# Cross-attention block: keys spread by two transfers, heads interleaved on even and odd partitions, three evictions on ScalarE, rows of the step in a new order

## The chip, the core and the metric

The kernel runs on one core of a Trainium2 chip. The metric is the device time of one execution in microseconds, and of several executions the median.

## The reference, cut to what matters

It is one transformer block with cross-attention, in float32. `x` (queries) and `ctx` (keys and values) have the shape 128 x 128 x 256: 128 batch rows, each with 128 tokens of width 256. There are 16 heads of width 16.

```python
q = (x @ Wq + bq).reshape(b, s, 16, 16).transpose(0, 2, 1, 3)
k = (ctx @ Wk + bk).reshape(b, s, 16, 16).transpose(0, 2, 1, 3)
v = (ctx @ Wv + bv).reshape(b, s, 16, 16).transpose(0, 2, 1, 3)
scores = einsum('bhqd,bhkd->bhqk', q, k) / sqrt(16)
scores = where(j < i, scores, -1e30)          # i query, j key
attn = softmax(scores, axis=-1)
attn[:, :, 0, :] = 0.0                        # query 0 has no keys
o = einsum('bhqk,bhkd->bhqd', attn, v).transpose(0, 2, 1, 3).reshape(b, s, 256)
x = layer_norm(x + o @ Wo + bo, ln1_g, ln1_b)
out = layer_norm(x + relu(x @ W1 + b1) @ W2 + b2, ln2_g, ln2_b)   # W1 256x1024
```

None of the biases and layernorm parameters is trivial.

## The kernel before

The 128 batch rows are taken two at a time: 64 pairs, each with 256 tokens. A pair passes through a pipeline some four steps long, so that one step works on the scores of pair p, on the context of pair p-2 or so, and on the feed-forward layers of pairs p-3 and p-4. Pairs 0 to 6 and the last are written out as special steps; all others run the same list, `ORDER`.

`ORDER` is a string of keys, written by hand. `step(p)` goes through it and calls, for each key, the piece of code behind it; `key-1` means that the piece is for pair p-1 of that count. Every engine executes its own instructions in exactly the written order and waits by semaphores for what it needs. So the list sets what stands ahead of what on each of TensorE (PE), VectorE (DVE), ScalarE (ACT), GpSimd (POOL) and on the DMA queue of SyncE (SP).

The dense products are made by a scheme with seven products of halves in place of eight (the class `Seven`). In the keys of the list a letter names the product and a digit which of its seven: `v` values, `o` attention output, `q` queries, `k` keys, `h` the first feed-forward layer, `w` the second. With a letter in place of the digit the key is an eviction of that product: `kk`/`kk2` keep a finished part (ACT), `ka`/`kb` add one bank to what was kept (DVE), `kr` is the rest, one 128x128 piece. `hk`/`hk2`/`hk5`, `ha`, `hb`, `hf` are the same for the first layer, and `re0` to `re3` and `ro0` to `ro3` its relu pieces. Each product has a fixed PSUM bank: first layer 0, 1, 2; keys 3; values 4; output 5; second layer 6; queries 7.

The attention of one step runs so:

- `scores` (L428): for all 16 heads of a pair, both batch rows, on TensorE in strips of 32 partitions. Only the blocks on and under the diagonal are made; the "high" halves (queries 64 to 127) go to banks 0 to 3, the "low" halves to banks 4 to 7.
- `mask...`, `max...`, `lowmax`, `eh...`, `el...`: mask, negated maxima (L1873, L1879), exponentials by head on ACT (L920), into `sm`.
- `turn0`, `turn1`, `turn2` (L521): the softmax weights are transposed in 32x32 blocks by DVE into the buffer `turned`, three instructions in a step. `turni` (L504) adds the inverse sums and `turnx` (L1935) blocks of x.
- `br0` to `br3`, `bring` (L540): sixteen DMAs of 128 KB on SP's queue move the blocks from `turned` to `brought`, each to the partitions where it belongs.
- `weigh` (L574, L584): the weights in `brought` by the values, on TensorE in banks 7 and 5; then `context` (L600) multiplies by the inverse sums, which also lie in `brought`, and ends the use of that buffer. The next pair's `bring` waits for it, and the next `turn` waits until `bring` has read `turned`.

The keys of a pair leave the product as `kr`, a tile with partition = feature (2 x 128 features), token along the free dimension. A strip of 32 partitions holds two heads, and the scores need each head by itself. So `spread` makes a tile `kT` in two halves: the even half with the odd heads set to zero, the odd half with the even heads set to zero. Both are made by multiplying `kr` with a column of zeros and ones, `half`: the even half by ACT (`ks`, L1267) and the odd half by POOL (`ks2`, L1272). The tile `kT` comes from a rotating pool.

Other lines that are named below: L1216 and L1221 `qa`, `qb` (queries, DVE), L1226 `qr`, L1243 the ACT evictions of keys, L1262 `kr`, L1256 and L1259 `ka` and `kb`, L1311 `vr` (last piece of the values), L1327 joins of a product with what was kept (`wr`, `wa` and others), L499 `recip`, L1908 `means`, L691 and L728 the normalizations on ACT and POOL (`norm1`, `norm2`), L753 `store` of the output, L92 and L99 the loads of tokens (`load`: four DMAs, `loadx`: one DMA of 512 KB every second step).

Of the kernel before, what the change touches and what calls it, by code (L numbers as in the profile page):

```python
# [19 lines left out]
def tile_cross_attention_block(  # L20
# [106 lines left out]
    wk = weight(Wk, "wk")  # L127
    wq = weight(Wq, "wq")
    c_first = loads.tile([P, 4, D], F32, tag="cb2", name="c_first", bufs=2)
    nc.scalar.dma_start(c_first[:, 0:2], c[0:2].rearrange("b p d -> p b d"))  # L130
    bk_c = column(bk, "bk_c")
    bq_c = column(bq, "bq_c")
# [50 lines left out]
    half4 = const.tile([P, 2, NS], F32, tag="half4", name="half4")  # L183
    half = const.tile([P, 2], F32, tag="half", name="half")
    nc.gpsimd.memset(half4, 1.0)
    for e in range(2):
        nc.gpsimd.affine_select(
            out=half4[:, e, :], in_=half4[:, e, :], compare_op=ALU.is_ge, fill=0.0,
            base=-DK * e, pattern=[[-32, NS]], channel_multiplier=1,
        )  # L190
        nc.gpsimd.affine_select(
            out=half4[:, e, :], in_=half4[:, e, :], compare_op=ALU.is_ge, fill=0.0,
            base=DK * e + DK - 1, pattern=[[32, NS]], channel_multiplier=-1,
        )
    nc.vector.tensor_reduce(half, half4, AX.X, ALU.add)
# [16 lines left out]
    WIDTH = (H + HH) * 32  # L212
    ROW = WIDTH + 2 * P
    turned_all = const.tile([P, NS * ROW + P], F32, tag="turned", name="turned")
# [108 lines left out]
    def project_keys(p, at=0):  # L323
        st = states[p]
        st["kT"] = proj.tile([P, KC, 2, TP], F32, tag="kT", name=f"kT_{p}")
        st["pk"] = project(wk, st["cT"], at_bank(at, f"pk_{p}") if p > 3 else bank(f"pk_{p}"), 6 if p < 2 else 0)
# [83 lines left out]
    def scores_both(p):  # L410
# [26 lines left out]
    def mask(p, hi, rs):  # L437
# [3 lines left out]
        if not hi and rs[0] == 0 and "both" in st:  # L441
            r = rs[0]
            at = (6, 4)[r // 2]
# [747 lines left out]
    class Queries(Seven):  # L1191
# [33 lines left out]
        def rest(self):  # L1225
            nc.vector.tensor_scalar(  # L1226
                self.q[:, 0, P:], self.a, QSCALE, bqs_c[:, 0:1], ALU.mult, ALU.add
            )

    class Keys(Seven):  # L1230

        def __init__(self, p, at):
            st = states[p]
            self.k = proj.tile([P, KC, TP], F32, tag="kr", name=f"kr_{p}", bufs=1)
            self.kT = st["kT"] = proj.tile([P, KC, 2, TP], F32, tag="kT", name=f"kT_{p}")
# [25 lines left out]
        def rest(self):  # L1261
            nc.vector.tensor_scalar(  # L1262
                self.k[:, 0, P:], self.a, bk_c[:, 0:1], None, ALU.add
            )

        def spread(self):
            nc.scalar.activation(  # L1267
# [1082 lines left out]
```

## Time and profile before

| | |
|---|---|
| median of 3 runs | 1527.7 us (1525.65 to 1528.93) |
| the profiled execution | 1528.17 us |
| its span | 1526.0 us, mean granted TensorE clock 0.993 |
| busy PE / weight loads | 1488.0 us (98% of the span) / 1415.2 us (93%) |
| busy DVE | 1410.1 us (92%) |
| busy ACT | 1299.1 us (85%) |
| busy POOL | 1320.8 us (87%) |
| DMA queue of SP | 61.7% of 16 engines' span, 199.58 MB |

The span is the time from the first to the last instruction that the profile has; the execution's own time holds 2.2 us more. The busy times of the engines overlap, and all are near the span: no engine is idle for long, so an average over the span does not tell which of them sets the pace. For that the prediction goes to one turn of the step and reads who waits for whom. In its rows a time in front is the start in us from the span's start, the number after it the busy time of the group, and `[0.18 <-DVE hT L1411]` says that the engine had waited 0.18 us, at the end of which that instruction released it. `<-` between tiles reads "made from".

### The profile page before, as it was taken

What the parts mean: (1) busy time and instruction counts of PE and PEld (TensorE: products, weight loads), DVE (VectorE), ACT (ScalarE), POOL (GpSimd) and SP (SyncE); (2) the same over time, 40 slices, a digit from 0 to 9 for tenths busy, and PEclk for the clock granted to TensorE, in tenths of its full rate; (3) what the DMA queues carried; (4) which work ended last, traced back from release to release, by engine and by line L of the source; (5) the groups of instructions that cost most, each with busy time, mean ns of one, the idle gap of its engine ahead of it and who ended that gap; (6) DMA issues with size and microseconds to landing.
All of it is one profiled execution on the core that took longest, in us unless ns stands there. A gap on an engine that the chain in (4) does not pass through costs nothing.

```text
span 1526.0 us, 56681 instructions
## 1 busy us (share of the span) xinstructions
PE 1488.0 (98%) x20711; PEld 1415.2 (93%) x20711; DVE 1410.1 (92%) x3397; ACT 1299.1 (85%) x5445; POOL 1320.8 (87%) x1877
## 2 busy tenths in 40 slices
PE   9999899999999999999999999999999999999898
PEld 7887799999999999999999999999999999999888
DVE  7987899999999999999999999999999999999577
ACT  6567798998998998998998998998998999999553
POOL 6876698998998998998998998998898898998767
PEclk9999899999999999999999999999999999999999
DMA  8366566766676766776766776666666666675251
GB/s 199 85 123 127 129 147 128 151 133 135 145 150 128 148 134 132 148 152 126 149 134 133 146 148 132 146 134 138 141 146 136 144 134 138 141 151 126 52 141 49
DMA packets 351298, 205.30 MB, mean 135 GB/s; under 512 B 277808, under 2 KB 319024, under 8 KB 351024
## 3 DMA queue, kind: packets, MB, share of 16 engines
q1 hardware_dynamic: 348736, 199.58, 61.7%
q8 instruction: 166, 2.72, 0.8%
q10 hardware_dynamic: 2288, 2.11, 0.6%
q14 instruction: 108, 0.88, 0.2%
HBM read 55.06 MB, written 18.09 MB: 48 GB/s over the span
## 4 chain that ended last, share of the span: by engine, by line
PE 79%; DVE 8%; POOL 4%; ACT 3%; SPq 2%; issue 2%; DMA 2%; DVEq 0%; POOLq 0%; ACTq 0%
PE banks L1175 40%; PE banks L1392 22%; PE banks L428 7%; PE banks L584 3%; DVE hT L1411 3%; PE banks L574 2%; SPq L540 2%; DVE turned L521 2%; ACT sm L920 1%; PE banks L858 1%; PE banks L960 1%; DMA brought<-turned 1%; PE banks L1072 1%; PE banks L288 1%; POOL sm L464 1%
## 5 line engine op out<-in xcount | busy, mean ns | idle before, releaser
L920 ACT ACTIVATE sm<-banks,nmx 128x128 f32<-128x128 f32 x944 | 355.2, 415 | 28.4 <-DVE nmx L1879 19.4
L920 ACT ACTIVATE sm<-sm,nmx 128x64 f32<-128x64 f32 x944 | 330.6, 425 | 0.0
L920 ACT ACTIVATION_READ_ACCUMULATOR sm<-sm,nmx 128x1 f32 x944 | 261.3, 277 | 0.0
L920 ACT ACTIVATION_READ_ACCUMULATOR sm<-banks,nmx 128x1 f32 x944 | 240.0, 254 | 0.0
L521 DVE STREAM_TRANSPOSE turned<-sm 128x1024 f32<-128x1024 f32 x186 | 226.1, 1219 | 7.8 <-DMA brought<-turned 5.7
L1868 POOL TENSOR_TENSOR hS<-hT 128x512 f32<-128x512 f32 x112 | 142.7, 1274 | 45.4 <-ACT hT L1433 26.6
L1175 PE MATMUL banks<-wt,hS 128*128 128x128 f32 x1344 | 177.7, 276 | 0.8 <-POOL hS L1868 0.8
L1392 PE MATMUL banks<-xS,w1t 128*128 128x128 f32 x1344 | 178.2, 276 | 0.0
L1175 PEld LDWEIGHTS banks<-wt,hS 128*128 128x128 f32 x1344 | 163.6, 192 | 1.0 <-POOL hS L1868 1.0
L1392 PEld LDWEIGHTS banks<-xS,w1t 128*128 128x128 f32 x1344 | 163.4, 192 | 0.0
L1879 DVE TENSOR_REDUCE nmx<-banks 128x4 f32<-128x512 f32 x224 | 146.1, 672 | 0.0
L1433 ACT ACTIVATE hT<-banks,b1e_c 128x256 f32<-128x256 f32 x168 | 72.4, 465 | 75.3 <-DVE hT L1431 54.5
L428 PE MATMUL banks<-kT,qT 32*64 32x128 f32 (+1 forms) x3840 | 118.8, 336 | 4.8 <-issue 2.3
L1392 PE MATMUL banks<-brought,w 128*128 128x128 f32 x896 | 118.4, 276 | 0.0
L428 PEld LDWEIGHTS banks<-kT,qT 32*64 32x64 f32 x3840 | 93.8, 132 | 20.7 <-issue 5.2
L1175 PE MATMUL banks<-w,hT 128*128 128x128 f32 x896 | 109.7, 276 | 2.2 <-DVE t L1327 1.9
L1272 POOL TENSOR_TENSOR kT<-kr,half 128x512 f32<-128x512 f32 x56 | 58.2, 1040 | 59.8 <-ACT hT L1433 41.3
L1392 PEld LDWEIGHTS banks<-brought,w 128*128 128x128 f32 x896 | 109.0, 192 | 0.0
L1175 PEld LDWEIGHTS banks<-w,hT 128*128 128x128 f32 x896 | 104.7, 192 | 2.7 <-DVE t L1327 2.1
L1421 ACT ACTIVATE hT<-hT,b1e_c 128x256 f32<-128x256 f32 x224 | 95.6, 497 | 1.4
L1873 DVE TENSOR_TENSOR banks<-banks,neg 128x256 f32<-128x256 f32 x224 | 89.9, 425 | 0.7 <-PE banks L428 0.4
L1900 DVE BATCH_NORM_STATS2 bsa<-t 128x6 f32<-128x256 f32 x224 | 83.2, 414 | 0.0
(330 smaller groups left out, 4936.9 us busy)
## 6 DMA issues: line engine op xcount, KB each, us to landing
brought<-turned SPq DMA_DIRECT2D x936, 128.0 KB, 2.4
out_dram<-t SPq DMA_DIRECT2D x63, 256.0 KB, 2.4
xb<-in_x_dram SPq DMA_DIRECT2D x124, 128.0 KB, 4.8
cb<-in_ctx_dram SPq DMA_DIRECT2D x124, 128.0 KB, 3.7
x<-in_x_dram SPq DMA_DIRECT2D x31, 512.0 KB, 4.2
brought<-turned SPq DMA_DIRECT2D x40, 96.0 KB, 2.2
w<-in_L_xattn_W_dram SPq DMA_DIRECT2D x2, 1024.0 KB, 8.1
brought<-turned ACTq DMA_DIRECT2D x8, 128.0 KB, 4.3
```

The costliest lines, as they stand in the source:

```text
L428: nc.tensor.matmul(st["sps", hi][r][s * HP : (s + 1) * HP, m * 2 * n : (m + 1) * 2 * n].rearrange("p (e j) -> p e j", e=2), st["qT"][strip ...
L521: nc.vector.transpose(turned[:, :, at : at + 256].rearrange("p j (n a) -> p n j a", a=32), states[p]["sm", hi].rearrange("p h j -> p (h j) ...
L920: nc.scalar.activation(sm[:, h, :], src, AF.Exp, bias=nmx[:, h : h + 1], scale=1.0, **({"accum_out": st["su"][:, at : at + 1]} if summed e ...
L1175: nc.tensor.matmul(out, left(k) if self.depth > 1 else left, right(k) if self.depth > 1 else right, start=(n == 1 and k == 0), stop=(k == ...
L1272: nc.gpsimd.tensor_tensor(self.kT[:, :, 1, :], self.k, half[:, 1:2, None].to_broadcast([P, KC, TP]), ALU.mult)
L1392: nc.tensor.matmul(ps[:, i * P : (i + 1) * P].rearrange("p (n a) -> p n a", a=32), left(i), right, start=(n in (1, 2, 5) and i == 0), stop ...
L1421: nc.scalar.activation(self.hT[:, f, at], self.hT[:, f, at] if src is None else src, AF.Relu, bias=b1e_c[:, f : f + 1], scale=1.0,)
L1433: nc.scalar.activation(out, src, AF.Relu, bias=bias, scale=1.0)
L1868: nc.gpsimd.tensor_tensor(c[:, n], left, right, how)
L1873: nc.vector.tensor_tensor(ps[:, :, HP:], ps[:, :, HP:], neg[:, 1, None, :].to_broadcast([P, 4, HP]), ALU.add)
L1879: nc.vector.tensor_reduce(states[p]["nmx", 1][:, 4 * b : 4 * b + 4], banks[:, b].rearrange("p (n j) -> p n j", j=P), AX.X, ALU.max, negate ...
L1900: nc.vector.bn_stats(states[p]["bs", p][:, at + s], states[q][t][:, s])
```

## The change

**Heads interleaved.** The weights Wk and Wq are loaded into a staging space (in `turned_all`, free at that time) and copied by ACT with their columns permuted, so that the two heads of a strip no longer stand on 16 partitions each but on the even and the odd partitions. The biases bk and bq are permuted by a small matmul with a permuted identity, `mixing`. `half` now is a column for the even and one for the odd partitions, made from the identity.

**Keys spread by two transfers.** `kT` is one of two fixed tiles, `kTs`, in turn. `ks` and `ks2` are no longer instructions of ACT and POOL; each is a DMA on SP's queue, which copies every second partition of `kr` to the same partitions of its half of `kT`. The partitions in between are not written.

**Three evictions to ScalarE.** `qr`, `kr` and `vr` go from DVE to ACT.

**Strips and masks.** The low halves of strip r go to bank 4 + r (before: 6, 7, 4, 5), and the eight groups of the scores are issued in another order of strips. The low halves of strips 0 and 1 are masked one by one (`maskA0`, `maskA1`) and those of 2 and 3 together (`maskB`), where it was the other way about.

**Rows ordered anew.** The list `ORDER` is written in another order.

```diff
+    given = turned_all[:, : 2 * KC * D].rearrange("p (w k n) -> p w k n", w=2, k=KC)
+    for i, w in enumerate((Wk, Wq)):
+        nc.sync.dma_start(given[:, i], w.rearrange("(k p) n -> p k n", p=P))
...
+    nc.vector.tensor_reduce(half, ident.rearrange("p (d e) -> p e d", e=2), AX.X, ALU.add)
+    mixing = turned_all[:, 2 * KC * D : 2 * KC * D + P]
+    nc.vector.tensor_copy(
+        mixing.rearrange("p (u d e) -> p u d e", d=DK, e=2),
+        ident.rearrange("p (u e d) -> p u d e", d=DK, e=2),
+    )
+    kTs = [const.tile([P, KC, 2, TP], F32, tag=f"kT{i}", name=f"kT{i}") for i in range(2)]
+    for i, w in enumerate((wk, wq)):
+        nc.scalar.copy(
+            w.rearrange("p k (u d e) -> p (k u) d e", d=DK, e=2),
+            given[:, i].rearrange("p k (u e d) -> p (k u) d e", d=DK, e=2),
+        )
...
-                at_bank(r if hi else (6, 7, 4, 5)[r], f"pss{hi}_{p}_{r}") for r in range(NS)
+                at_bank(r if hi else 4 + r, f"pss{hi}_{p}_{r}") for r in range(NS)
...
-            (two, 0, 0), (one, 1, 0), (two, 0, 1), (one, 1, 1),
-            (two, 1, 0), (two, 1, 1), (one, 0, 0), (one, 0, 1),
+            (one, 0, 0), (two, 1, 0), (one, 0, 1), (two, 1, 1),
+            (one, 1, 0), (one, 1, 1), (two, 0, 0), (two, 0, 1),
...
     class Queries(Seven):
         def rest(self):
-            nc.vector.tensor_scalar(
-                self.q[:, 0, P:], self.a, QSCALE, bqs_c[:, 0:1], ALU.mult, ALU.add
-            )
+            self.put(0, 1, self.a)
     class Keys(Seven):
-            self.kT = st["kT"] = proj.tile([P, KC, 2, TP], F32, tag="kT", name=f"kT_{p}")
+            self.kT = st["kT"] = kTs[p % 2]
         def rest(self):
-            nc.vector.tensor_scalar(
-                self.k[:, 0, P:], self.a, bk_c[:, 0:1], None, ALU.add
-            )
-        def spread(self):
-            nc.scalar.activation(
-                self.kT[:, :, 0, :], self.k, AF.Identity, bias=0.0, scale=half[:, 0:1]
-            )
-        def spread_on_pool(self):
-            nc.gpsimd.tensor_tensor(
-                self.kT[:, :, 1, :], self.k, half[:, 1:2, None].to_broadcast([P, KC, TP]), ALU.mult
-            )
+            self.put(0, 1, self.a)
+        def spread(self, e):
+            nc.sync.dma_start(self.kT[e::2, :, e, :], self.k[e::2])
     class Values(Seven):
         def rest(self):
-            nc.vector.tensor_copy(self.to(1, 0), self.cut(self.a))
+            nc.scalar.copy(self.to(1, 0), self.cut(self.a))
...
-        weigh ks-1 ks2-1 re3-2 hf-2 re2-2 vs-1 wr-2 context scores hs2-1 ro0-2 br3 maskB2 ro2-2
+        weigh re0-2 ro3-2 recip-1 vr-1 re1-2 wr-2 res1-1 loadx-2 turni-1 re2-2 store-2 re3-2
+        context scores vs-1 br3 maskA0 ro2-2 oc2 maskA1 ro1-2 add3 v1 oc0 maskB xs0-1 o1 hs0-1
```

In `put` (L1243 for the keys) ACT adds the bias while it reads the bank. The lines of the changed kernel stand 4 to 9 away from those of before: L521 becomes L525, L540 L544, L428 L432, L1175 L1179, L1392 L1385, L1327 L1320, L1411, L1414 and L1417 become L1404, L1407 and L1410, L1431 L1424, L499 L503, L504 L508, L1908 L1909, L1935 L1936, L753 L757, L574 L578, L584 L588, L600 L604.

**How the order moves.** First VectorE, from the end of one step's list to the beginning of the next, before the change: from the second layer's join (`t<-banks,t`) and the first `turn` (`turned<-sm`) on. `rs` are the inverse sums, `hT` the hidden layer, `kr` the keys, `qT` the queries, `vz` the values.

```order
L1327 TENSOR_TENSOR t_29_11746<-banks,t_29_11746 128x256
L521 STREAM_TRANSPOSE turned<-sm_11672 128x8x4x32
L499 RECIPROCAL rs_11919<-su_11739 128x32
L521 STREAM_TRANSPOSE turned<-sm_11672 128x8x4x32
L504 STREAM_TRANSPOSE turned<-rs_11919 128x4x4x32
L1411 TENSOR_TENSOR hT<-banks,hT 128x4x128
L1259 TENSOR_TENSOR kr_11889<-banks,kr_11889 128x2x128
L1256 TENSOR_TENSOR kr_11889<-banks,kr_11889 128x128
L1935 STREAM_TRANSPOSE turned<-x_32_11936 128x4x4x32
L1226 TENSOR_SCALAR qT_11734<-banks,bqs_c 128x128
L1431 TENSOR_SCALAR hT<-banks,b1e_c 128x256
L1311 COPY vz_175<-banks 128x4x2x16
```

And after it, at the same place:

```order
L1320 TENSOR_TENSOR t_29_11704<-banks,t_29_11704 128x256
L525 STREAM_TRANSPOSE turned<-sm_11640 128x8x4x32
L1320 TENSOR_TENSOR t_29_11704<-banks,t_29_11704 128x128
L1909 BN_AGGR mv_11858<-bsa_11770 128x2 x4
L1261 TENSOR_TENSOR kr_11806<-banks,kr_11806 128x2x128
L1258 TENSOR_TENSOR kr_11806<-banks,kr_11806 128x128
L1220 SCALAR_TENSOR_TENSOR qT_11752<-banks,qT_11752 128x128
L1225 SCALAR_TENSOR_TENSOR qT_11752<-banks,qT_11752 128x2x128
L525 STREAM_TRANSPOSE turned<-sm_11640 128x8x4x32 x2
L1404 TENSOR_TENSOR hT<-banks,hT 128x4x128
L1407 TENSOR_TENSOR banks<-banks,hT 128x512
L1410 TENSOR_TENSOR hT<-banks,hT 128x4x128
```

Between the first `turn` and what follows stand now a second join, the four aggregates (`mv<-bsa`), and the evictions of keys and queries, which stood before `turn` or later; the other two `turn`s come directly after them, and `hb` (L1407), earlier in the step before, stands between `ha` and `hf`. `qr`, `kr` and `vr` are gone, and `turni` and `recip` come later.

Second, the DMA queue of SP, two steps long, before (`x`, `xb`, `cb` are tokens, `out_dram` the output):

```order
L540 DMA brought<-turned 32x1024 x16
L92 DMA cb_9752<-in_ctx_dram 32x32x32 x4
L753 DMA out_dram<-t_21_8914 128x2x256
L540 DMA brought<-turned 32x1024 x16
L99 DMA x_10099<-in_x_dram 128x4x256
L92 DMA xb_10107<-in_x_dram 32x32x32 x4
L753 DMA out_dram<-t_22_9267 128x2x256
L540 DMA brought<-turned 32x1024 x16
```

And after:

```order
L544 DMA brought<-turned 32x1024 x16
L1267 DMA kT_171<-kr_11100 64x2x256 x2
L92 DMA cb_11205<-in_ctx_dram 32x32x32 x4
L99 DMA x_11279<-in_x_dram 128x4x256
L757 DMA out_dram<-t_25_10292 128x2x256
L544 DMA brought<-turned 32x1024 x16
L1267 DMA kT_170<-kr_11454 64x2x256 x2
L92 DMA xb_11559<-in_x_dram 32x32x32 x4
```

Before, the loads stood directly behind the brings, and the store alone ahead of the next ones. Now the two transfers of keys stand behind the brings, then the loads, then the store.

Third, TensorE, from `h7` (the first row) to `weigh`, before (the first layer's products have `xS` or `brought` with `w1t` or `w`; those with `xT`, `cT` and `cc` are queries, values and keys):

```order
L1392 MATMUL banks<-xS_11046,w1t 128x128 x4
L1175 MATMUL banks<-xT_10745,wqt 128x128
L1175 MATMUL banks<-wvt,cT_10694 128x128
L1175 MATMUL banks<-cc_11154,wkt 128x128
L1392 MATMUL banks<-brought,w1t 128x128 x4
L1175 MATMUL banks<-cT_11049,wkt 128x128
L1392 MATMUL banks<-xS_11046,w_132 128x128 x4
L574 MATMUL banks<-brought,vd_181 32x64 x8
```

And after:

```order
L1385 MATMUL banks<-xS_10987,w1t 128x128 x4
L1385 MATMUL banks<-brought,w_132 128x128 x4
L1385 MATMUL banks<-xS_10987,w_132 128x128 x4
L1179 MATMUL banks<-wvt,cT_10702 128x128
L1179 MATMUL banks<-xT_10725,wqt 128x128
L1385 MATMUL banks<-brought,w1t 128x128 x4
L578 MATMUL banks<-brought,vd_180 32x64 x8
```

`h4` (`brought` with `w1t`) stood three products behind `h7`, with `k4` and `h3` behind it, and is now the last before `weigh`; ahead of it come `h2`, `h3`, `v4` and `q4`, and `k4` stands ahead of `h7`.

More of the change, by code (lines that the diff above doesn't have):

```diff
@@ L440, in mask @@
         no = neg.rearrange("p u j -> p (u j)") if hi else neg[:, 1, :]
-        if not hi and rs[0] == 0 and "both" in st:
+        if not hi and len(rs) == 2 and rs[0] and "both" in st:
             r = rs[0]
-            at = (6, 4)[r // 2]
+            at = 4 + r
             nc.vector.tensor_tensor(
@@ L1467, in tile_cross_attention_block @@
     empty(4)
+    pb = bank("pb_qk")
+    nc.tensor.matmul(
+        pb[:, : 2 * KC], mixing,
+        b_given.rearrange("p w k -> p (w k)"), start=True, stop=True,
+    )
+    b_c = const.tile([P, 2, KC], F32, tag="b_c", name="b_c")
+    nc.vector.tensor_copy(b_c.rearrange("p w k -> p (w k)"), pb[:, : 2 * KC])
+    bk_c, bq_c = b_c[:, 0], b_c[:, 1]
     bkh = const.tile([P, KC, 2], F32, tag="bkh", name="bkh")
@@ L1724, in fifth @@
         exponential(p, 1, ONE)
-        mask(p, 0, A)
+        mask(p, 0, B)
         maximum(p, 0, ALL)
@@ L1762, in fall_in @@
         load_ahead(p)
-        mask(p, 0, B)
+        mask(p, 0, A)
         mask_high(p, 0, 1)
@@ L1807, in sixth @@
         combine_w1()
-        mask(p, 0, B)
+        mask(p, 0, A)
         mask_high(p, 0, 1)
```

61 lines of the change are left out of this document (25 added, 36 removed).

## The prediction

> **What bounds the kernel now.** I read the busy time by stretches first, to find where the time lies. The columns after the stretch and its length are the busy time and count of PE, PE's weight loads, DVE, ACT and POOL, then the granted clock, the DMA share and GB/s.
>
> ```profile
> 190.95:1402.54 1211.59, 1198.29 (x17385) 1159.79 (x17384) 1164.97 (x2917) 1103.08 (x4771) 1090.79 (x1590) 1.00 0.67 140
> 739.86:762.56 22.70, 22.52 (x330) 21.89 (x329) 21.91 (x57) 20.84 (x91) 20.57 (x30) 1.00 0.73 152
> ```
>
> The first row holds 53 turns of the ordered step, from one start of `weigh` to another: 1211.59 / 53 = 22.86 us a turn. The second row is a single turn of 22.70 us. PE is busy for nearly all of it, and DVE, ACT and POOL for over nine tenths; the clock is 1.00. So 80% of the time is one step repeated, and it pays only to ask what closes that step's loop. PE's own rows come next: TensorE at the end of that turn.
>
> ```profile
> 759.78 0.39 PE L1175 MATMUL banks<-cc,wkt 128*128 128x128 f32 x2
> 760.35 1.16 PE L1392 MATMUL banks<-brought,w1t 128*128 128x128 f32 x8 [0.18 <-DVE hT L1411]
> 761.35 0.39 PE L1175 MATMUL banks<-cT,wkt 128*128 128x128 f32 x2
> 761.57 1.06 PE L1392 MATMUL banks<-xS,w 128*128 128x128 f32 x8
> 762.56 0.43 PE L574 MATMUL banks<-brought,vd 128*32 128x64 f32 x16
> 764.04 0.57 PE L428 MATMUL banks<-kT,qT 32*64 32x128 f32 x9
> ```
>
> Two rows of a product take 0.22 us (761.35 to 761.57), so eight take 0.89. The pair at 759.78 took 0.57, that is 0.35 too much, and the eight rows of `h4` took 1.00, 0.11 too much: `h4` waits for VectorE's `ha` (L1411), which reads the bank that `h4` adds to. That is PE's only stop in the turn. Without it the turn is 22.70 - 0.45 = 22.25 us, PE's floor.
>
> VectorE in the same turn (it goes in order, so the distance between two starts is an instruction's price):
>
> ```profile
> 741.71 0.41 DVE L600 TENSOR_TENSOR cxT<-banks,brought 128x256 f32<-128x256 f32 x1
> ...
> 754.97 0.41 DVE L1221 SCALAR_TENSOR_TENSOR qT<-banks,qT 128x256 f32<-128x256 f32 x1
> 755.29 0.37 DVE L1908 BATCH_NORM_AGGREGATE mv<-bsa 128x2 f32<-128x6 f32 x4
> 755.74 0.62 DVE L1327 TENSOR_TENSOR t<-banks,t 128x128 f32<-128x128 f32 x2
> 756.28 1.24 DVE L521 STREAM_TRANSPOSE turned<-sm 128x1024 f32<-128x1024 f32 x1
> 757.44 0.31 DVE L499 RECIPROCAL rs<-su 128x32 f32<-128x32 f32 x1
> 757.67 1.19 DVE L521 STREAM_TRANSPOSE turned<-sm 128x1024 f32<-128x1024 f32 x1
> 758.78 0.66 DVE L504 STREAM_TRANSPOSE turned<-rs 128x512 f32<-128x512 f32 x1
> 759.61 0.69 DVE L1411 TENSOR_TENSOR hT<-banks,hT 128x512 f32<-128x512 f32 x1 [0.17 <-ACT x L691]
> 760.22 0.42 DVE L1259 TENSOR_TENSOR kr<-banks,kr 128x256 f32<-128x256 f32 x1
> 760.55 0.28 DVE L1256 TENSOR_TENSOR kr<-banks,kr 128x128 f32<-128x128 f32 x1
> 760.75 0.70 DVE L1935 STREAM_TRANSPOSE turned<-x 128x512 f32<-128x512 f32 x1
> 761.37 0.31 DVE L1226 TENSOR_SCALAR qT<-banks,bqs_c 128x128 f32<-128x128 f32 x1
> 761.62 0.48 DVE L1431 TENSOR_SCALAR hT<-banks,b1e_c 128x256 f32<-128x256 f32 x1
> 762.02 0.28 DVE L1311 COPY vz<-banks 128x128 f32<-128x128 f32 x1
> 762.22 0.34 DVE L1262 TENSOR_SCALAR kr<-banks,bk_c 128x128 f32<-128x128 f32 x1
> 762.48 1.24 DVE L521 STREAM_TRANSPOSE turned<-sm 128x1024 f32<-128x1024 f32 x1
> 763.64 0.66 DVE L1417 TENSOR_TENSOR hT<-banks,hT 128x512 f32<-128x512 f32 x1
> 764.21 0.28 DVE L1327 TENSOR_TENSOR t<-banks,x1b 128x128 f32<-128x128 f32 x1
> ```
>
> The first `turn` starts 14.57 us after `context` (741.71 to 756.28); `context` comes again 8.13 us later (764.41, one join of 0.20 after 764.21). Between them lies a second loop, over the DMA queue. `context` frees `brought`; then SP issues the 16 `bring` transfers; the first `turn` overwrites what they read and must await the last landing. SP's rows of four turns, then who waited for whom (us in total, times, longest), the issue-to-landing medians and the semaphore instructions ahead of `turn`:
>
> ```profile
> 742.18 10.99 SPq L540 DMA_DIRECT2D brought<-turned  x16
> 764.88 11.56 SPq L540 DMA_DIRECT2D brought<-turned  x16
> 810.91 10.91 SPq L540 DMA_DIRECT2D brought<-turned  x16
> 833.61 12.01 SPq L540 DMA_DIRECT2D brought<-turned  x16
> ```
> ```profile
> SPq L540 <- DVE cxT L600: 235.3, 54, 5.3
> DVE turned L521 <- DMA brought<-turned: 5.7, 4, 3.3
> ```
> ```profile
> brought<-turned SPq DMA_DIRECT2D x936, 128.0 KB, 2.4
> x<-in_x_dram SPq DMA_DIRECT2D x31, 512.0 KB, 4.2
> ```
> ```profile
> L521 DVEq EVENT_SEMAPHORE  x246: 21/50/1778, 53.5 to 1459.4; - x123
> ```
>
> The sixteen start 0.47 us after `context` (742.18 against 741.71) and take 11.37 us in the mean; the last is issued a sixteenth (0.7) before the row's end and lands 2.4 later: 13.1 us from first issue to last landing. The waits on about four semaphore instructions of 0.05 us add some 0.2. So `turned` is free 13.8 us after `context`, 0.8 before VectorE gets there at 14.57. That agrees with only four waits of `turn` for the DMA in the whole run. The DMA loop now closes in 0.47 + 13.1 + 0.2 + 8.13 = 21.9 us, below the 22.70 of the PE and DVE pair. It is slack of 0.8, not more.
>
> **The change, part by part.** The spreads and the evictions, by instruction:
>
> ```profile
> L1267 ACT ACTIVATE kT<-kr,half x56: 712/723/726, 166.8 to 1425.5; 128x512 f32<-128x512 f32 x56
> L1272 POOL TENSOR_TENSOR kT<-kr,half x56: 1038/1040/1042, 166.9 to 1425.4; 128x512 f32<-128x512 f32 x56
> ```
> ```profile
> L1243 ACT ACTIVATE kr<-banks,bk_c 128x128 f32<-128x128 f32 x168 | 59.6, 416 | 1.4 <-PE banks L1175 1.4
> ```
>
> POOL loses 1.04 of its 20.57 us. ACT loses 0.72 and gains three evictions of at most 0.42: at most +0.5 on 20.84, inside its 1.9 us of idle time. VectorE loses `qr` 0.25, `vr` 0.20 and `kr` 0.26: 0.71 us. None of the three is worth anything by itself unless VectorE's loop gets shorter.
>
> The key transfers. After `k4` PE still runs `h7`, `h2`, `h3`, `v4`, `q4`, `h4` (36 rows at 0.11: 4.0 us) and `weigh` (762.56 to 764.04: 1.48), so 5.5 us lie between the last key product and the first score. The path is an eviction (0.4), the first issue (0.7), the second with its landing (2.4): 3.5. Even with the slower landing of 4.2 it is 5.3, still inside. I price it at nothing, covered by those products; if the cover were gone the scores would stop. SP is idle from the end of the brings until then, and the two issues push the loads (four, then `x` every second turn, then `store`) to the last 4 us before `context`. `store` has its POOL work done by then, since POOL's list is shorter.
>
> The strip order and the bank order of the low scores are a relabelling with the same matmuls: nothing on PE. What it gives is that banks 0 and 1 are written fifth and not second, while their `relu` evictions now start after `hf`; one pays for the other.
>
> The order. On PE, `h7` is now followed by `h2`, `h3`, `v4`, `q4` (2.2 us) before `h4`, so `ha` has its time and the stop of 0.45 us can go: PE's floor is within reach. What is late next is the DMA loop, since VectorE's list between the first `turn` and `context` has grown. By the starts above: `turn` 1.16, W's join 0.20, the four aggregates 0.45, `kb` 0.33, `ka` 0.20, `qa` 0.20, `qb` 0.32, two `turn`s 1.11 and 1.16, `ha` 0.61, `hb` 0.61, `hf` 0.57, `turnx` 0.62, `re0` 0.40, `recip` 0.23, `wr` 0.20, `turni` 0.6: 9.0 us against 8.13. (Out went 0.71 of evictions and a wait; in came the aggregates, `qa`, `qb`, `hb` and a join, 1.8.) Ahead of `turn` VectorE has 14.57 less those 1.8: 12.8 us, so it arrives 1.0 us before the landing at 13.8 and waits, in most turns. The loop is then 0.47 + 13.1 + 0.2 + 9.0 = 22.77 us by round terms. Two of them are high: the aggregates' 0.45 holds a wait of 0.08 for PE, and `turn` hides part of the semaphore work when they come early. I take 22.70. With the shortest of the four bring rows (10.91) it is 22.3, PE's floor; with the longest (12.01) 23.4.
>
> PE follows: `ha` ends 5.74 us after `turn` starts, then `h4` and `weigh` (1.0 + 1.48), 8.2, before `context` at 9.0. PE gets slack in place of its stop, and part of its scattered lost time (22.86 against 22.70) disappears in it. That is why I set 22.70 against 22.86 and not against 22.70.
>
> Start and end: two copies of the weights, one small product for the biases (all beside loads) and a first mask that in the last step waits for all scores: 0 to 2 us, I take +1. Sum: 53 x (22.70 - 22.86) + 1 = -7.5 us. The profiled execution took 1528.17 (span 1526.0 and 2.2 around it), 0.5 above the median of 1527.7; from the median I predict **1520 us**.
>
> **Rivals.** (1) The floor: the brings land as early as VectorE comes, PE never stops, 22.25 a turn, with the same scattered loss 22.41: 53 x -0.45 + 1 = -23, 1505 us. For it: the short bring rows. Against: VectorE's arrival at 12.8 is 1 us early. (2) Slower, by one mechanism: the loads now stand directly before the brings on SP's queue, where before a store alone did. `x` lands 4.2 us after its issue, a bring 2.4; were those 1.8 us passed on to the last landing every second turn, the loop would be 0.9 longer; half of it is worked off, if sixteen brings are issued more slowly than they move. At +0.45 the turn is 23.15: 53 x 0.29 + 1 = +16, 1544 us. It decides from +0.16 us a turn. Against it: the loads get 4 us of lead. The Trainium skill, page "DMA: Bandwidth & Descriptors", section "Queues, rings and completion order", has a rule for this side: "On each SDMA engine descriptors are consumed in ring order". By it the loads' bytes go first, and the time would be that of this rival; no row of before has loads right ahead of brings, so the trace cannot say how much is left at the last landing. (3) No change: the loop comes out at 22.8 to 22.9, 1527 us. (4) The keys land late: over 2.0 us more than priced, scores and all behind them wait, some 1550 us.
>
> **How the numbers follow.** Likeliest, the DMA loop at 22.5 to 22.8: 0.50 (its own range 1510 to 1525). Floor: 0.12. No change: 0.18. Loads ahead of brings: 0.16. Late keys or another new wait: 0.04. The range runs from inside the floor case to inside the slower one: 1502 to 1540. Within 0.2% (about what a measurement of this kernel tells from no change) is 1524.6 to 1530.8. Faster 0.58 (floor, and most of the likeliest), same 0.22, slower 0.20.
>
> **What would show it.** Right: the first `turn` of a step waits for the DMA in most turns, 0.5 to 1.5 us each, where it was four times; `h4` no longer waits for `ha` by 0.35 in every turn; the mean turn is 22.5 to 22.8; POOL about 1 us lighter a turn; scores without waits for `kT`. Wrong: `turn` never waits and the turn is 22.3 (floor); bring rows or landings longer than 11.4 and 2.4 (loads ahead); or PE waiting at the scores.

## The result and the profile after

The changed kernel takes 1569.12 us (median of 4 runs, 1559.15 to 1571.77), the kernel before 1527.77 in the same comparison: a ratio of 1.026, 95% interval 1.0212 to 1.0309. It is slower by 41 us, where 7.5 us less had been forecast.

The same view as before, 53 turns of the ordered step from one start of `weigh` to another:

```profile
188.48:1441.36 1252.88, 1201.25 (x17385) 1152.61 (x17384) 1124.24 (x2757) 1120.80 (x4876) 1038.66 (x1538) 1.00 0.64 147
```

A turn takes 1252.88 / 53 = 23.64 us, 0.78 more than before. 53 times 0.78 is 41.3 us, the beginning is 2.5 us shorter and the end 0.3 longer; together that is the difference of the spans (1565.1 against 1526.0). The engines' own work moved as it was priced: in a turn VectorE 0.77 less, GpSimd 0.98 less, ScalarE 0.33 more. TensorE is busy for 22.67 of 23.64 us where it was for 22.61 of 22.86. So the loss is waiting. SP's rows of one turn show where it begins (start, duration of the issues, what is transferred, how many), with the starts of `weigh` and `context` below them:

```profile
944.66 1.35 SPq L1267 DMA_DIRECT2D kT<-kr  x2
946.06 3.76 SPq L92 DMA_DIRECT2D cb<-in_ctx_dram  x4
949.86 1.19 SPq L99 DMA_DIRECT2D x<-in_x_dram  x1
951.14 1.25 SPq L757 DMA_DIRECT2D out_dram<-t  x1
952.51 10.82 SPq L544 DMA_DIRECT2D brought<-turned  x16
```
```profile
948.18 0.43 PE L578 MATMUL banks<-brought,vd 128*32 128x64 f32 x16
950.08 0.39 DVE L604 TENSOR_TENSOR cxT<-banks,brought 128x256 f32<-128x256 f32 x1
```

`context` of this turn started at 950.08. The first bring could have left some 0.47 us later, as before the change, but SP was still issuing `x` and then `store`, and so the brings start 2.4 us after it. In the mean the first bring starts 1.30 us after `context` in the 27 turns with `x` and 0.66 in the 26 without. All of this stands behind the first row: the transfers of the keys wait for the evictions of the keys, and the loads wait behind them in the queue. SP's waits say the same:

```profile
SPq L1267 <- DVE kr L1258: 248.8, 56, 5.6
SPq L544 <- DVE cxT L604: 16.5, 22, 3.8
```

SP waits 248.8 us for the keys, once in each step, with the loads behind it. For `context` it waited 54 times and 235.3 us before the change; now it does so 22 times. In the other turns it comes to the brings when `context` is already over.

Then VectorE in the same turn, and TensorE (start, busy time, what waited for whom in brackets):

```profile
962.48 0.41 DVE L1320 TENSOR_TENSOR t<-banks,t 128x256 f32<-128x256 f32 x1
965.45 1.25 DVE L525 STREAM_TRANSPOSE turned<-sm 128x1024 f32<-128x1024 f32 x1 [2.56 <-DMA brought<-turned]
966.62 0.25 DVE L1320 TENSOR_TENSOR t<-banks,t 128x128 f32<-128x128 f32 x1
966.80 0.36 DVE L1909 BATCH_NORM_AGGREGATE mv<-bsa 128x2 f32<-128x6 f32 x4
967.07 0.39 DVE L1261 TENSOR_TENSOR kr<-banks,kr 128x256 f32<-128x256 f32 x1
```
```profile
964.79 0.61 PE L1385 MATMUL banks<-xS,w1t 128*128 128x128 f32 x4
966.93 1.16 PE L1179 MATMUL banks<-wt,hT 128*128 128x128 f32 x8 [1.53 <-DVE t L1320]
967.92 0.39 PE L1179 MATMUL banks<-cT,wkt 128*128 128x128 f32 x2
```

The first `turn` waits 2.56 us for the landing of the brings. Over the whole run `turn`'s waits are put down to these:

```profile
DVE turned L525 <- DMA brought<-turned: 37.5, 20, 3.4
DVE turned L525 <- ACT hT L1398: 24.9, 11, 2.9
DVE turned L525 <- ACT sm L924: 11.2, 9, 1.8
DVE turned L525 <- ACT kr L1245: 9.4, 8, 2.4
DVE turned L525 <- ACT qT L1207: 3.4, 5, 0.8
```

The first row alone would say that `turn` waits in a third of the turns. But a wait is put down to the last semaphore event before its end, and ScalarE has many: the exponentials that the first `turn` reads were done 2.1 us or more before it in every turn, and in every one of the 53 turns it starts at most 0.66 us behind a landing (0.28 in the mean). So the rows belong together. VectorE is idle just before the first `turn` in 49 of 53 turns, 1.48 us a turn in the mean, where it was 0.04 before the change.

From the first `turn` to the next `context` VectorE then works without a gap: 0.03 us of idle time a turn. The DMA loop closes over SP, the transfers and VectorE's own list.

Directly behind the waiting `turn` stands a join of the second layer (`wa`, 966.62), and TensorE needs this join for `w4` (966.93): it stops for 1.53 us. Over the whole run (waits of the weight loads and of the matmuls; the two overlap):

```profile
PEld banks L1179 <- DVE t L1320: 41.9, 40, 2.5
PE banks L1179 <- DVE t L1320: 36.6, 37, 2.3
PEld banks L432 <- issue: 25.7, 21, 2.1
PE banks L432 <- issue: 16.4, 20, 1.8
```

The last two rows are another stop: TensorE halts in the middle of the scores and waits for nothing that the profile names. Before the change these rows were

```profile
PEld banks L428 <- issue: 5.2, 11, 0.9
PE banks L428 <- issue: 2.3, 5, 0.7
```

The loop over the DMA queue, taken apart from the traces (means over 51 turns, in us; the first three lines add up to the turn, within rounding; the lines below the turn are idle times and no terms of that sum, and those of VectorE are over 53 turns):

| | before | after | loads_behind | join_first | loads_and_join | x_behind | before_late_loads |
|---|---|---|---|---|---|---|---|
| `context` to the first bring | 0.48 | 0.99 | 0.46 | 0.95 | 0.47 | 0.63 | 0.94 |
| first bring to the first `turn` | 14.23 | 13.82 | 13.65 | 13.94 | 13.66 | 13.79 | 14.74 |
| first `turn` to the next `context` | 8.14 | 8.80 | 8.80 | 8.34 | 8.45 | 8.83 | 8.07 |
| the turn | 22.86 | 23.61 | 22.91 | 23.22 | 22.57 | 23.25 | 23.75 |
| VectorE idle before the first `turn` | 0.04 | 1.48 | 1.06 | 1.05 | 0.58 | 1.00 | 0.31 |
| TensorE's stops among the scores | 0.07 | 0.45 | 0.23 | 0.44 | 0.21 | 0.52 | 0.49 |
| TensorE's stops at `w4` | 0 | 0.77 | 0.39 | 0 | 0 | 0.41 | 0 |

The columns behind "after" are the experiments. In nearly all turns of the changed kernel VectorE waits for the brings at one end of the loop and has no idle time at the other, so TensorE's two stops are not what sets the turn: TensorE needs 22.10 us in the shortest turn and has to stop somewhere when the loop takes 23.61.

### The profile page after: what moved, and what is told of

It is laid out like the page before. It is cut to its first block, busy times and chain, and to the rows that moved or that the text cites. A ratio compares the mean times of both kernels' runs of the same rounds, so it can differ in the third digit from the quotient of the medians.

```text
span 1565.1 us, 56376 instructions
## 1 busy us (share of the span) xinstructions
PE 1486.7 (95%) x20713; PEld 1404.5 (90%) x20713; DVE 1366.5 (87%) x3231; ACT 1319.0 (84%) x5559; POOL 1265.2 (81%) x1816
## 5 line engine op out<-in xcount | busy, mean ns | idle before, releaser
L924 ACT ACTIVATE sm<-banks,nmx 128x128 f32<-128x128 f32 x944 | 334.7, 377 | 17.6 <-DVE nmx L1880 8.3
L924 ACT ACTIVATE sm<-sm,nmx 128x64 f32<-128x64 f32 x944 | 321.2, 367 | 0.0
L525 DVE STREAM_TRANSPOSE turned<-sm 128x1024 f32<-128x1024 f32 x186 | 223.7, 1227 | 87.6 <-DMA brought<-turned 37.5
L924 ACT ACTIVATION_READ_ACCUMULATOR sm<-banks,nmx 128x1 f32 x944 | 205.8, 218 | 0.0
L924 ACT ACTIVATION_READ_ACCUMULATOR sm<-sm,nmx 128x1 f32 x944 | 205.7, 218 | 0.0
L1179 PE MATMUL banks<-wt,hS 128*128 128x128 f32 x1344 | 178.5, 276 | 0.6 <-DVE t L1320 0.6
L1385 PE MATMUL banks<-xS,w1t 128*128 128x128 f32 x1344 | 178.3, 276 | 0.0
L1179 PEld LDWEIGHTS banks<-wt,hS 128*128 128x128 f32 x1344 | 164.3, 193 | 0.9 <-issue 0.9
L1385 PEld LDWEIGHTS banks<-xS,w1t 128*128 128x128 f32 x1344 | 164.3, 193 | 0.1
L1880 DVE TENSOR_REDUCE nmx<-banks 128x4 f32<-128x512 f32 x224 | 153.3, 684 | 3.9
L432 PE MATMUL banks<-kT,qT 32*64 32x128 f32 (+1 forms) x3840 | 123.5, 334 | 19.6 <-issue 16.4
L750 POOL TENSOR_TENSOR t<-t,g_r 128x512 f32<-128x512 f32 x62 | 79.1, 1277 | 75.3 <-ACT t L732 75.3
L432 PEld LDWEIGHTS banks<-kT,qT 32*64 32x64 f32 x3840 | 85.8, 131 | 46.8 <-issue 25.7
L1179 PE MATMUL banks<-w,hT 128*128 128x128 f32 x896 | 119.5, 276 | 2.3 <-DVE t L1320 1.4
L1414 ACT ACTIVATE hT<-hT,b1e_c 128x256 f32<-128x256 f32 x224 | 101.8, 501 | 23.3 <-DVE hT L1410 22.4
L1385 PE MATMUL banks<-brought,w 128*128 128x128 f32 x896 | 118.8, 276 | 0.0
L1179 PEld LDWEIGHTS banks<-w,hT 128*128 128x128 f32 x896 | 109.8, 193 | 2.7 <-DVE t L1320 1.5
L1385 PEld LDWEIGHTS banks<-brought,w 128*128 128x128 f32 x896 | 109.6, 193 | 0.0
L1245 ACT ACTIVATE kr<-banks,b_c 128x128 f32<-128x128 f32 x224 | 78.5, 376 | 33.8 <-PE banks L1179 33.1
L1179 PE MATMUL banks<-wt,hT 128*128 128x128 f32 x448 | 63.7, 285 | 32.7 <-DVE t L1320 32.3
```

The costliest lines, as they stand in the source:

```text
L432: nc.tensor.matmul(st["sps", hi][r][s * HP : (s + 1) * HP, m * 2 * n : (m + 1) * 2 * n].rearrange("p (e j) -> p e j", e=2), st["qT"][strip ...
L525: nc.vector.transpose(turned[:, :, at : at + 256].rearrange("p j (n a) -> p n j a", a=32), states[p]["sm", hi].rearrange("p h j -> p (h j) ...
L750: nc.gpsimd.tensor_tensor(t2, t2, g2_r[:, None, :].to_broadcast([P, 2, D]), ALU.mult)
L924: nc.scalar.activation(sm[:, h, :], src, AF.Exp, bias=nmx[:, h : h + 1], scale=1.0, **({"accum_out": st["su"][:, at : at + 1]} if summed e ...
L1179: nc.tensor.matmul(out, left(k) if self.depth > 1 else left, right(k) if self.depth > 1 else right, start=(n == 1 and k == 0), stop=(k == ...
L1245: nc.scalar.activation(self.k[:, m, s * P : (s + 1) * P], src, AF.Identity, bias=bk_c[:, m : m + 1], scale=1.0,)
```

## The experiments

Theory L: the token loads, which stand ahead of the brings on SP's queue, cost the time. Theory J: the join behind the waiting `turn` does. Theory K: the two key transfers themselves do. The order of the rows is shown as the neighbours in the list; `...` stands for the rest of the new list.

**Loads behind the brings (loads_behind).**

```diff
-br0 eh3
+br0 loadx-1 load-1 eh3
-res1-1 loadx-2 turni-1
+res1-1 turni-1
-norm1 load-1 finish1
+norm1 finish1
...
```

> The changed kernel, with the token loads (four DMAs, and the one of 512 KB every second step) moved on SP's queue from between the keys' transfers and the store to directly behind the brings; nothing else. In the changed kernel a turn takes 23.61 us in the mean: the first bring starts 0.99 us after context (0.48 before the change), 13.3 us pass from it to the last landing (13.05 before), and TensorE stops 0.45 us a turn among the scores and 0.77 at w4, the product that waits for the join behind the first turn. Theory L (the loads ahead of the brings cost it): first bring back at 0.5, 13.05 to the last landing, no stops among the scores, 0.8 us a turn less, 22.8 us, 1527 us in all. Theory J (the join behind the waiting turn costs it, the loads are harmless): stops at w4 stay at 0.5 or more, 23.3 us or more, 1552 or more. Theory K (the keys' two transfers cost it): no change, 1569.

Measured: 1528.51 us, ratio to the kernel before 0.9996 (0.998 to 1.0011). That is theory L's number. The first bring is back at 0.46, and from the first bring to the sixteenth it takes 10.84 us where it took 11.02 in the changed kernel (10.47 before). What L had not right is that half of the stops remain, both among the scores (0.23) and at `w4` (0.39). SP's rows at the same place:

```profile
946.48 1.36 SPq L1267 DMA_DIRECT2D kT<-kr  x2
948.25 0.38 SPq L757 DMA_DIRECT2D out_dram<-t  x1
952.35 11.36 SPq L544 DMA_DIRECT2D brought<-turned  x16
963.75 0.58 SPq L99 DMA_DIRECT2D x<-in_x_dram  x1
```

Between `store` and the brings SP now has 3.7 us to spare.

**Join ahead of the first turn (join_first).**

```diff
-h6-1 turn0
+h6-1 wa-1 means turn0
-k3 wa-1 h5-1 hk2-1 means kb
+k3 h5-1 hk2-1 kb
```

> The changed kernel, with VectorE's second join of the second layer and the four aggregates moved from directly behind the first turn to directly ahead of it; nothing else. Theory J: w4 no longer waits (0.77 us a turn), the next stop is at k4, which waits for ka, 0.6 us earlier than w4's stop reached; 22.9 to 23.0 us a turn, 1532 us. Theory L: the loop over the DMA queue is as long as before up to the first turn, and from there to context the shorter list of VectorE (8.2 for 8.8) gives back 0.3 at most; stops among the scores stay at 0.45; 23.3 us, 1553 us. Theory K: 23.3 to 23.6.

Measured: 1545.38 us, ratio 1.01 (1.0073 to 1.0127): between the two. `w4` does not wait any more and the next stop is at `k4`, as J said. But the gain is not `w4`'s: the time from `turn` to `context` falls by 0.46 us (8.80 to 8.34), and 0.46 us is what the moved join and the four aggregates take in VectorE's list (0.18 and 0.28). Ahead of `turn` they fill time in which VectorE waited; behind it they lengthened the loop. The late bring and the stops among the scores stay, as L said. So the place of the join is a second term, by VectorE's list and not, as J had it, by TensorE's wait.

**Both (loads_and_join).**

```diff
-br0 eh3
+br0 loadx-1 load-1 eh3
-h6-1 turn0
+h6-1 wa-1 means turn0
...
```

> Both moves together: loads directly behind the brings, join and aggregates ahead of the first turn. Theory L with J as a second term: 0.5 + 13.05 + 0.4 + 8.4 = 22.35 us a turn, near TensorE's floor of 22.25: 1503 to 1510 us, faster than both kernels. If one of the two carries all of the loss: the same as the better of the two single moves.

Measured: 1511.23 us, ratio 0.9876 (0.9856 to 0.9896), 22.57 us a turn. The two moves give 0.70 and 0.39 us a turn by themselves and 1.04 together: they nearly add up. This version is faster than both kernels.

```profile
188.84:1385.86 1197.02, 1187.94 (x17387) 1147.82 (x17386) 1129.47 (x2757) 1117.08 (x4876) 1040.64 (x1538) 1.00 0.67 153
```

TensorE is busy for 22.41 of 22.59 us a turn, and the shortest turn is 22.10. VectorE still waits before the first `turn` in 40 of 53 turns, 0.58 us in the mean: the DMA loop is near TensorE's floor, but in most turns it is still the later one.

**Keys spread by the engines again (spread_engines, best_engines).** The order is the changed one. The body of `spread` is ScalarE's multiplication by `half` for even and GpSimd's for odd partitions.

```diff
-            nc.sync.dma_start(self.kT[e::2, :, e, :], self.k[e::2])
+            if e == 0:
+                nc.scalar.activation(
+                    self.kT[:, :, 0, :], self.k, AF.Identity, bias=0.0, scale=half[:, 0:1]
+                )
+            else:
+                nc.gpsimd.tensor_tensor(
+                    self.kT[:, :, 1, :], self.k, half[:, 1:2, None].to_broadcast([P, KC, TP]), ALU.mult
+                )
```

> The changed kernel, with the two key transfers made again by ScalarE (even partitions) and GpSimd (odd partitions), each multiplying by a column of zeros and ones; order of the rows as changed. SP then issues 16 brings, the loads and the store, and nothing of the keys' wait holds back the loads, which leave directly behind the brings. Theory L: as with the loads moved, 22.8 us a turn, 1527 us; 0.2 more where the spreads delay an eviction on ScalarE. Theory K (the transfers' own traffic and issues cost it): clearly below the run with the loads moved, 22.5 or less, 1510. Theory J: stops at w4 stay, 23.3 us or more.

Measured: 1526.79 us, ratio 0.9983 (0.9968 to 0.9997), within its noise the same as with the loads moved. Theory K falls: the transfers' own issues and bytes cost nothing that can be seen. They cost only by holding the loads back on the queue. Once more, with both moves of rows:

> Loads directly behind the brings, join and aggregates ahead of the first turn, and the keys spread by ScalarE and GpSimd as before the change. With the transfers this order took 1511 us, 22.57 a turn. Theory N (the two transfers are worth nothing by themselves, hidden or not): 1511 within 4. Theory K (their issues and bytes lengthen the loop): 1500 to 1505, since the store also leaves earlier. A gain by the transfers (ScalarE and GpSimd get 0.7 and 1.0 us): 1515 or more.

Measured: 1509.95 us, ratio 0.9879 (0.9863 to 0.9894), as with the transfers. The transfers are worth nothing and cost nothing there.

**Only the load of 512 KB behind the brings (x_behind).**

```diff
-br0 eh3
+br0 loadx-1 eh3
-res1-1 loadx-2 turni-1
+res1-1 turni-1
...
```

> The changed kernel, with the one load of 512 KB (every second step) moved from between the keys' transfers and the store to directly behind the brings; the four small loads stay ahead of the store. Theory L by issues (SP needs about 0.7 us for each transfer, and the row of two key transfers, four loads, x and store that starts 3.5 us before weigh ends after context): the turns with x lose their 0.5 us, first bring 0.65 after context in all turns, 23.35 us a turn, 1556 us. Theory L by bytes (the small loads, in rows of 32x32 elements, clog the engines): the same or less gain, stops among the scores stay at 0.45. If only x mattered: as with all loads moved, 22.9 us, 1529.

Measured: 1549.53 us, ratio 1.0149 (1.0113 to 1.0184). The turns with `x` took 23.86 us and those without it 23.35 in the changed kernel; now both take 23.25. The first bring comes at 0.63. But the stops among the scores stay at 0.52. With the small loads moved as well (loads_behind) they are 0.23 and the turn is 0.34 shorter. Nearly all of that stands in the loop's first two terms (0.63 to 0.46 and 13.79 to 13.65). So `x` and the small loads both cost as issues ahead of the brings, 0.36 and 0.34 us a turn; the small loads also go with the longer stops among the scores, but that those stops cost time in this kernel is not shown.

**The loads of the kernel before moved the same way (before_late_loads).**

```diff
-el7 loadx w7-1 cc3 qb load-1 el5
+el7 w7-1 cc3 qb el5
-store-1 norm2
+store-1 loadx load-1 norm2
```

> The kernel before the change, with the token loads moved on SP's queue from directly behind the brings to directly behind the store, so that they stand ahead of the next brings as in the changed kernel; nothing else. Theory L in two parts: (a) stops among the scores come also here, 0.3 to 0.5 us a turn for 0.07; (b) the first bring of the turns with the 512 KB load starts up to 0.8 us late, hidden by the slack of the DMA loop (1.18 us between last landing and first turn). Together 23.1 to 23.3 us a turn, 1541 to 1550. If the stops among the scores are the changed kernel's own (its strip order, its key transfers), they don't come: 22.9, 1529.

Measured: 1573.88 us, ratio 1.0303 (1.0285 to 1.0321). This edit alone, without any part of the change, costs as much as the whole change, though not by the same terms. The stops among the scores come here too (0.49), so they are not of the changed strip order or of the key transfers. One turn, SP and TensorE:

```profile
687.75 0.42 SPq L99 DMA_DIRECT2D x<-in_x_dram  x1
688.22 4.11 SPq L92 DMA_DIRECT2D xb<-in_x_dram  x4
692.76 2.03 SPq L540 DMA_DIRECT2D brought<-turned  x1
```
```profile
691.19 1.68 PE L428 MATMUL banks<-kT,qT 32*64 32x128 f32 x58
695.62 0.44 PE L428 MATMUL banks<-kT,qT 32*64 32x128 f32 x6 [2.75 <-issue]
```

The four small loads take 4.11 us to issue and TensorE stops for 2.75 us in the scores. The time is above the expected 1541 to 1550. The slack of the loop did not hide the late bring: the first bring starts 1.40 us after `context` in the turns with `x` (0.48 in the others), and the first `turn` now waits in 16 of 53 turns where it waited in 3. And here, where VectorE set the pace together with TensorE, the stops do reach it: its masks wait for the scores.

```profile
DVE sm L444 <- PE banks L428: 24.9, 15, 3.6
PEld banks L1392 <- DVE hT L1411: 34.5, 56, 2.0
```

The first was 3.6 us in 7 waits in the kernel before, the second 23.1 us in 56. VectorE is idle for 1.74 us a turn where it was for 0.88; 0.40 of that is the masks, 0.27 the `turn`s. The granted clock is a third part. It never fell in these turns of the kernel before; here it was 0.5 in four stretches, 17.1 us in all, of which this is one:

```profile
696.25:699.65 3.40, 3.40 (x18) 3.40 (x18) 3.40 (x6) 1.83 (x10) 3.40 (x6) 0.50 0.70 152
```

Each of them begins within 0.7 us of the end of a stop among the scores (steps of 2.15 to 3.25 us), and they lie in the four longest turns, 26.4 to 29.1 us, where the median turn is 23.40. A fifth step of 2.47 us has none behind it, so it is not shown that the stops bring the clock down. The changed kernel has one such stretch (3.4 us), in its longest turn of 26.50. By an estimate, half speed for 17.1 us costs 9 us at most, so the clock is a part of what lies above the expectation and not all of it.

**The three evictions back on VectorE (best_dve)**: `qr`, `kr`, `vr`, both moves kept.

```diff
 class Values(Seven):
         def rest(self):
-            nc.scalar.copy(self.to(1, 0), self.cut(self.a))
+            nc.vector.tensor_copy(self.to(1, 0), self.cut(self.a))
...
```

> Loads and join moved as before, and the three evictions qr, kr and vr back on VectorE in the places where ScalarE has them. If VectorE's list from the first turn to context closes the loop, qr and vr lie in it (0.45) and kr too (0.26): up to 0.7 us a turn more, 23.2, 1545 us, where the loop over the DMA queue binds; half of it where TensorE's floor hides the rest, 1530. If ScalarE binds instead, no change or a gain: 1511 or less.

Measured: 1532.52 us, ratio 1.0038 (1.0025 to 1.0051), some 21 us more than with ScalarE. From `turn` to `context` it takes 8.99 us for 8.45. The evictions on ScalarE are worth their while because VectorE's list behind `turn` is a term of the loop.

**`k4` behind `h7` (best_k4, best_k4_hk5)**, both moves kept.

```diff
-turn1 k4 el3 h7-1 kr hk5-1
+turn1 el3 h7-1 k4 kr hk5-1
```

> Loads and join moved as before, and k4 on TensorE moved behind h7, so that ka has 0.44 us more before TensorE needs it. k4's stop (0.15 us a turn in the mean) goes down; the loop from the first turn to context is then VectorE's own list, 8.0 to 8.25 for 8.45: 22.4 us a turn, 1503 us. If the keys become late by it (0.44 us later), stops among the scores rise above 0.21.

Measured: 1527.34 us, ratio 0.9995 (0.9983 to 1.0008), 16 us slower than without this edit, against the expectation. TensorE has a new stop in every turn, and ScalarE's rows tell why:

```profile
599.85 0.37 ACT L1245 ACTIVATE kr<-banks,b_c 128x128 f32<-128x128 f32 x1 [0.62 <-PE banks L1179]
600.12 0.58 ACT L1401 COPY hT<-banks 128x512 f32<-128x512 f32 x1
```
```profile
599.65 1.06 PE L1385 MATMUL banks<-brought,w 128*128 128x128 f32 x8
600.84 1.13 PE L1385 MATMUL banks<-xS,w 128*128 128x128 f32 x8
```

`kr` now waits 0.62 us for `k4`; `hk5` (L1401) stands behind it on ScalarE, and `h3` (600.84) needs the bank that `hk5` reads. Eight rows of a product take 0.89 us, here 1.19 pass: the stop of 0.30. With `hk5` ahead of `kr`:

```diff
-h7-1 k4 kr hk5-1
+h7-1 k4 hk5-1 kr
```

> As the last run (loads and join moved, k4 behind h7), and on ScalarE the eviction hk5 moved ahead of kr. In the last run kr, which waits for k4, stood ahead of hk5, and h3 waits for the bank that hk5 reads: TensorE stopped 0.30 us in every turn (shortest turn 22.47, before that edit 22.10). If that is the cause, the stop is gone, the shortest turn is 22.1 again and the mean 22.4 to 22.5: 1502 to 1508 us. If it isn't, 1527 again.

Measured: 1511.51 us, ratio 0.9892 (0.987 to 0.9914). The stop is gone and the shortest turn is 22.10 again, as said; but the mean of 22.61 is no better than without the two edits. `k4`'s own wait was not what closed the loop, as VectorE's list without idle time says too.

## Why the prediction was wrong, by its own steps

**The DMA loop as the next bound: right.** Its sum had four terms, and the changed kernel's loop has the same four. Taken to `turn` they were 0.47 + 13.3 + 9.0 = 22.77, taken as 22.70; measured 0.99 + 13.82 + 8.80 = 23.61. The missing 0.91 us is 0.52 in the first term, 0.52 in the second, 0.07 that had been taken off the sum, less 0.20 in the last. Its first sign came true: the first `turn` waits in 49 of 53 turns, 1.48 us in the mean, where 0.5 to 1.5 had been said.

**The first term is the step that failed.** The prediction let the two key issues push the loads into the last 4 us before `context`, and under its second rival said that the loads get 4 us of lead. Its own price denied it: an issue takes 0.7 us, and behind the wait for the keys stand two key transfers, four loads, `x` and `store`, eight issues, 5.6 us. The row starts 3.5 us before `weigh` and `context` comes 1.9 after it: 5.4 us. There was no lead in the turns with `x`, and every issue that took longer than 0.7 (four took 3.76 us above) made the first bring later: 1.30 us after `context` in these turns and 0.66 in the others, where 0.47 was priced. The stall was priced for the keys alone, not for what is queued behind them. With the loads behind the brings the turn is 22.91 and the time 1528.51 us, near the forecast. Rival 2 named the place, but as bytes passed on to the last landing and at less than half the loss.

**The second term** was made of the mean landing of turns in which nobody waited for it, and 0.2 for the semaphores. Now that `turn` waits, 13.65 us pass even with the loads moved away. Some 0.35 was missing for that: from the first issue to the sixteenth it takes 10.84 us where 10.7 had been taken, from there to the last landing 2.53 for 2.4, and from the landing to `turn` 0.28 for 0.2. The loads add 0.17, and the brings are issued slower by as much (11.02 us from the first to the sixteenth).

**The last term** was right, in size (8.80 for 9.0) and in whose work it is: VectorE's list, with 0.03 us of idle time a turn. TensorE gets slack in place of its stop, as the prediction said: no wait of `h4`'s rows for `ha` is left. What it did not say is where the slack would show. `w4` needs `wa`, which stood ahead of `turn` and now stands behind it: TensorE stops there for 0.77 us a turn and then runs 5.3 us to `weigh` without a gap. That looks like a loss, but with the loads moved the stop is half as long (0.39) and the term is 8.80 as before; without it (join_first) the term falls by the moved work alone. The join and the aggregates in this list were priced (0.20 and 0.45), but not asked about: they need not stand behind `turn`, and join_first shows that this was worth 0.39 us a turn.

**The stops among the scores** were in no step. They are 0.45 us a turn for 0.07. No term of the loop holds them, and the changed kernel's time is accounted for without them; in before_late_loads they do cost time.

**Right:** keys ready in time, 0.67 us before `weigh` in the mean of the 14 turns in which the trace has both landings; the transfers and the relabelled strips free; GpSimd 1 us lighter; the evictions worth something only through VectorE's list. Start and end gave 2.2 us where 1 us was to be lost; no run looks into why.

By the Trainium skill, page "DMA: Bandwidth & Descriptors", section "Queues, rings and completion order", descriptors are consumed in ring order on each engine. The traces agree for what follows directly: `store`, now issued behind the loads, lands after 4.7 us where it took 2.4. At the end of the brings nothing of it is left: where the trace has the sixteenth's landing, 2.60 us pass from its issue to the last landing (33 turns), 2.70 before the change (47 turns). So the loads' bytes are worked off by then, against what rival 2 took from this rule.

```profile
out_dram<-t SPq DMA_DIRECT2D x63, 256.0 KB, 4.7
```

## What the runs showed of the hardware

By what the trace shows, the stops among the scores are TensorE waiting for its own instructions. The trace has the packets that fetch code; the page counts them:

```profile
q8 instruction: 166, 2.72, 0.8%
```

They are blocks of 16 KB, 138 of them in the 53 turns. TensorE's 41,426 weight loads and matmuls come to 250 for each of the 166; no other engine has more than 5,600 instructions, so the queue is taken to be TensorE's. In six runs (before, after, loads_behind, x_behind, loads_and_join, before_late_loads) there are 98 steps of over 0.33 us between two score matmuls: 6, 21, 16, 24, 16 and 15. Each of the 98 ends 1.17 to 1.66 us after the end of such a packet. Of the score matmuls without a stop 9 to 14% lie 1.1 to 1.9 us behind one. The other runs agree: 88 more such steps in five of them, 1.07 to 1.62 us behind a packet, and 15 of 24 in best_dve, where the other nine, of 0.33 to 0.35 us, follow an eviction by ScalarE. The packets themselves took about 1.1 us before and after the change; so it seems that they come late. With the small loads ahead of the brings, and so in flight at the scores, the mean of these steps is 1.20 us (after), 1.19 (x_behind) and 1.74 (before_late_loads); with the loads behind the brings it is 0.58 (before), 0.74 (loads_behind) and 0.73 (loads_and_join). What holds the packets the trace does not show, nor why 16 stops are left with the loads behind the brings where the kernel before had 6.

The Trainium skill, page "Runtime: NRT & Kernel Launch", section "Instruction fetch mechanics", says that instructions are refilled in 16 KiB blocks over a DMA queue of the sequencer's own and that the cost of crossing a block is "mostly hidden". The block size agrees. Hidden it was with 0.07 us a turn before; with the loads in flight it was 0.45, up to 2.1 us at one stop in the changed kernel, and 3.25 in the kernel before with late loads.

## What to carry to other kernels

When an issue on an in-order queue is made to wait, count the whole row behind it at its own price per issue, up to the next transfer that matters: here eight issues of 0.7 us filled a gap of 5.4, and moving five of them gave back 41 us. When a loop is moved onto an instruction that will wait, work behind it on that engine is paid in full and work ahead of it fills the wait: 0.46 us of join and aggregates, moved ahead of the waiting transpose, gave back 0.39 us a turn. A stop of the busiest engine is not yet a loss: TensorE stopped for 0.77 us a turn at `w4`, and the loop that made it stop ran elsewhere. Look which engine has no idle time between its waits. And a row of the waits that names one releaser can be a part of the whole: the transpose waited 1.48 us a turn, and the row that names the transfers has less than half of it.
